# A four-layer graph network on one core: another order for the last six chunks of its attention stage

## The chip, the cores and the metric

The kernel runs on one core of a Trainium2 chip. The metric is device time in microseconds (us), the median of the runs shown. A core has five instruction queues that matter here: TensorE (PE in the profile), VectorE (DVE), ScalarE (ACT), GpSimd (POOL) and SyncE (SP), which issues the DMAs. Each queue is worked off strictly in order, and semaphores hold an instruction until what it reads is there and what it overwrites has been read.

## The reference

The input `x` is 128 graphs of 64 nodes with 256 features, all float32, and one 64 x 64 adjacency for all. Four layers follow each other, each as `x = x + layer(relu(layernorm(x)))`:

```python
# layer 0: graph convolution with two batch norms
# layer 1: two graph convolutions, then LSTMs over windows of 1, 2, 3 and 4 nodes
# layer 2: causal attention, one head
q, k, v = split(h @ Wqkv);  s = q @ k.T / 16 + adj;  s = where(causal, s, -1e30)
x = x + (softmax(s) @ v) @ Wo
# layer 3: attention with 4 heads of 64, masked where adj == 0
q, k, v = split(h @ W);     s = q @ k.T / 8 + (0 if adj else -inf)
x = x + softmax(s) @ v
```

The change touches only the last part of layers 2 and 3.

## The kernel before

The rows of `x` are cut into 16 chunks of 512 rows (8 graphs), and `x` stays on chip. Layers 0 and 1 end at about 1490 us. Then an attention stage takes each chunk through layers 2 and 3. It is written as some 50 small named steps (`q5`, `score3`, `turn3` and so on), each a function of the chunk number. Three strings say in which order the steps are recorded: FIRST once, ROUND eight times (chunks 4 to 11, some 21 us each), LAST once. A word `score3+13` in LAST is the step `score3` for chunk 13. The instructions stand under a manual schedule, so each engine's queue has them in the order of the words; nothing else reorders them.

What a chunk passes through, with the engine of each step and the line by which the profile shows it:

- Layer 2. `norm2` (statistics on VectorE, L159 and L160; an inverse square root on GpSimd, L99 and L100), `apply2` (nmr on VectorE, L185; four activations on ScalarE, L187), `chan2` (eight transposes on TensorE, L240; copies on VectorE and ScalarE). `sums2` makes four differences on GpSimd (L327 to L330) for a product of seven block products instead of eight: `wz`, `w5`, `w6`, `w3`, `w7`, `w4` (TensorE, L1773 and L1776) with copies on ScalarE (L1786), and additions on VectorE (L1789) in `w7`, `w11`, `w12`. Queries and values lie in `qv`. `score2` (TensorE, L1836; mask and maximum on VectorE, L1839 and L1648; subtraction on GpSimd, L1649), `exp2` (ScalarE), `divide2` (sum, reciprocal and product on VectorE, L1653, L1658, L1659), `turn2` (two transposes on TensorE, L1668; copy on ScalarE, L1672), `out2` (TensorE, L1867; VectorE adds to `xs`, L1870).
- Between the layers. `norm3a`, `norm3b`, `apply3` (L2003, L2004, L99, L185, L187), `square3` (VectorE transposes 32 x 32 squares, L286, and SP stores the result to DRAM, far_h<-mid, L261), `load3` (SP reads it back turned, hT<-far_h, four DMAs, L268), `keep` and `back` (SP stores `xs` and reads it back in another row order, far_x<-xs, L261, and x<-far_x, four DMAs, L279).
- Layer 3. `sums_h` (GpSimd, four differences), then `qa`, `q5`, `q6`, `q3`, `qc`, `qd` (TensorE, L1938) with `c11`, `c12` (VectorE), and `va`, `v5`, `v6`, `v3`, `v7`, `v4` (TensorE, L2062) with `v11`, `v12` (VectorE, L2075). `score3` (TensorE, L2025; VectorE, L2031 and L1648; GpSimd, L1649), `exp3`, `sum3`, `divide3`, `turn3` (eight transposes, two copies on ScalarE), `out3` (TensorE, L2142), `store` (VectorE, L2157, and one DMA out, L2158).
- Chunk 15 ends otherwise: plain products `q30`, `k30`, `q31`, `k31` (L1526), `v3a`, `v3b` (L1519), `score3h`, and the rest in two halves (`exp3a` to `storeb`; L2192, L2208, L2213, L2229, L2230).

Buffers are few: all PSUM products share eight banks; `x` (the row order for the output) has two buffers, so a third `back` waits until a `store` has read its predecessor; `td`, `td2`, `mid`, `qk` and layer 2's `hT` have one each, most others two.

Of the kernel before, what the change touches and what calls it, by code (L numbers as in the profile page):

```python
# [19 lines left out]
def kernel(  # L20
# [2203 lines left out]
    def store(c, t):  # L2224
# [3 lines left out]
        for r in range(2):  # L2228
# [16 lines left out]
               w11+1 sum3-3 v6-2 w12+1 v12-3 divide3-3 load3-1 qc-2 v5-2 v11-2 out2+0 v7-2 qd-2 sums2+2  # L2245
               back-3 norm3a+0 q3-2 norm3b+0 turn3-3 c12-2 v4-2 wz+2 apply3+0 score2+1 exp2+1 score3-2
               out3-3 store-3 divide2+1 w6+2 w5+2 qa-1"""
    LAST = """sums_h+10 va+10 turn2+12 square3+11 exp3+9 w11+13 back+9 v3+9 v11+10 w7+13 load3+11 sum3+9
              v5+10 v12+9 v6+10 q6+10 w3+13 w4+13 divide3+9 q5+10 norm2+14 w12+13 v7+10 turn3+9 qc+10
              c11+10 apply2+14 out2+12 norm3a+12 qd+10 back+10 v4+10 score2+13 q3+10 c12+10 norm3b+12 v3+10  # L2250
              sums_h+11 exp2+13 divide2+13 out3+9 store+9 va+11 score3+10 turn2+13 qa+11 chan2+14 apply3+12
              out2+13 v6+11 c11+11 q5+11 norm3a+13 sums2+14 wz+14 v5+11 q6+11 square3+12 norm2+15 v12+10
              q3+11 w5+14 w6+14 keep+12 exp3+10 qc+11 w3+14 sum3+10 w7+14 divide3+10 qd+11 load3+12 v7+11
              v3+11 c12+11 w4+14 back+12 turn3+10 v4+11 apply2+15 w12+14 v11+11 keep+13 sums_h+12 w11+14
              norm3b+13 score3+11 out3+10 qa+12 va+12 c11+12 q5+12 apply3+13 store+10 score2+14 v5+12
              chan2+15 q6+12 v11+12 keep+11 exp2+14 sums2+15 exp3+11 square3+13 divide2+14 back+11 q3+12
              v6+12 wz+15 v12+11 qc+12 turn2+14 v7+12 c12+12 sum3+11 w6+15 qd+12 w11+15 out2+14 load3+13
              score3+12 w5+15 v4+12 sums_h+13 w7+15 w3+15 divide3+11 qa+13 norm3a+14 w4+15 w12+15 norm3b+14
              exp3+12 turn3+11 sum3+12 score2+15 q5+13 apply3+14 out3+11 exp2+15 q6+13 q3+13 v3+12 va+13
              v5+13 store+11 divide3+12 turn3+12 v6+13 square3+14 divide2+15 c11+13 v12+12 turn2+15 qc+13  # L2260
              out2+15 norm3a+15 norm3b+15 v7+13 out3+12 qd+13 load3+14 v3+13 v4+13 c12+13 sums_h+14
              apply3+15 keep+15 score3+13 va+14 qa+14 square3+15 q5+14 store+12 v11+13 q6+14 v6+14 c11+14
              q3+14 v5+14 c12+14 exp3+13 qc+14 sum3+13 qd+14 divide3+13 load3+15 score3+14 v12+13 keep+14
              v7+14 exp3+14 v3+14 turn3+13 q30+15 v11+14 sum3+14 k30+15 q31+15 v12+14 divide3+14 k31+15
              turn3+14 score3h+15 out3+13 exp3a+15 sum3a+15 v3a+15 back+13 v4+14 divide3a+15 exp3b+15
              back+15 v3b+15 turn3a+15 out3+14 store+13 sum3b+15 divide3b+15 back+14 out3a+15 storea+15
              turn3b+15 store+14 out3b+15 storeb+15"""
    assert (NCH, SUP) == (16, 2)

    def run(order, c):  # L2270
        for name in order.split():
            i = max(name.find("+"), name.find("-"))
            steps[name[:i]](c + int(name[i:]))

    with tc.manual_schedule(engines={mybir.EngineType.PE, mybir.EngineType.DVE,
# [3 lines left out]
        for c in range(4, 12):  # L2279
            run(ROUND, c)  # L2280
        run(LAST, 0)
    close_l2()
# [49 lines left out]
```

## Time and profile before

| what | value |
|---|---|
| median of 3 runs | 1844.11 us (1843.9 to 1846.07) |
| the profiled execution | 1844.12 us; its span 1842.3 us |
| busy over the span | PE 98%, DVE 73%, ACT 58%, POOL 36% |
| granted TensorE clock | 0.998 |
| LAST: first matmul to end of span | 1724.98 to 1842.3 |

The first row is what a change is judged by; the profile shows one execution from its first to its last instruction, and 1.8 us lie around its span. A timeline line gives the start, the duration, the engine, the line, the operation with its operands' names, how many instructions are merged, and in brackets the idle time before it with its releaser. A duration is that of a pipelined instruction, so the distance between two starts says more of an engine's pace than the durations do. A line of the chain gives start, duration, and what worked or waited.

### The profile page before, as it was taken

The numbers are of one execution on the slowest core, as the hardware profiler recorded it, in microseconds if no ns is written. First come the engines' busy times: TensorE is split into PE (matmuls) and PEld (weight loads), VectorE is DVE, ScalarE is ACT, GpSimd is POOL, SyncE is SP. The second block draws the span as 40 slices with busy tenths as digits, with TensorE's granted clock in tenths as the row PEclk, the third lists the DMA queues.
The fourth block names the chain that finished last, engine by engine and source line by source line (L and its number), as shares of the span: only waits on it lengthen the run. The fifth ranks groups of instructions, "written<-read, shape, count | busy, mean of one in ns | idle before, by whom it ended". The sixth has DMA issues, their size and how long they took to land.

```text
span 1842.3 us, 41656 instructions
## 1 busy us (share of the span) xinstructions
PE 1812.8 (98%) x15847; PEld 1530.5 (83%) x15847; DVE 1353.4 (73%) x3475; ACT 1061.0 (58%) x2538; POOL 656.5 (36%) x916
## 2 busy tenths in 40 slices
PE   8999999999999999999999999999999999999997
PEld 6876866997897899799699789879968887998885
DVE  5768857567667777777777777777676677888997
ACT  5766636557457466665655746556565654554553
POOL 5865823223223322422321332232232215444442
PEclk9999999999999999999999999999999999999999
DMA  3213651233443342243443434324154146544444
GB/s 117 70 58 139 221 218 53 81 115 126 133 143 127 115 153 81 98 146 110 149 154 122 149 115 161 110 95 147 41 172 149 64 110 202 155 139 139 139 139 138
DMA packets 113416, 234.54 MB, mean 127 GB/s; under 512 B 11713, under 2 KB 77121, under 8 KB 113217
## 3 DMA queue, kind: packets, MB, share of 16 engines
q1 hardware_dynamic: 112320, 230.02, 38.3%
q8 instruction: 125, 2.05, 0.5%
q0 software_dynamic: 320, 1.05, 0.2%
q10 hardware_dynamic: 576, 0.82, 0.1%
q14 instruction: 75, 0.61, 0.1%
HBM read 164.21 MB, written 67.63 MB: 126 GB/s over the span
## 4 chain that ended last, share of the span: by engine, by line
PE 88%; DVE 5%; ACT 2%; POOL 2%; DMA 1%; issue 1%; SPq 0%; ACTq 0%; DVEq 0%; POOLq 0%
PE x L1186 23%; PE z L1186 11%; PE y L1186 6%; PE y L1133 4%; PE x L1368 4%; PE y L1368 3%; PE u L948 3%; PE v L934 3%; PE x L1133 3%; PE X L1938 2%; PE X L436 2%; PE X L512 2%; PE z L1133 2%; PE v L2062 2%; PE X L1773 1%
## 5 line engine op out<-in xcount | busy, mean ns | idle before, releaser
L1101 ACT ACTIVATE l_gates<-l_gates,bias 128x256 f32<-128x256 f32 (+4 forms) x528 | 238.1, 498 | 210.9 <-DVE l_gates L1195 109.7
L1186 PE MATMUL x<-xd,wset 128*128 128x128 f32 (+2 forms) x1152 | 254.9, 303 | 0.8 <-ACT l_gates L1192 0.8
L1186 PE MATMUL x<-l_hd,wset 128*128 128x128 f32 (+2 forms) x1152 | 254.6, 303 | 0.0
L1252 POOL TENSOR_TENSOR l_gates<-l_gates 128x512 f32<-128x512 f32 (+2 forms) x48 | 75.3, 1569 | 368.1 <-ACT l_gates L1101 368.1
L1195 DVE TENSOR_TENSOR l_gates<-l_gates,x 128x128 f32<-128x128 f32 (+2 forms) x384 | 121.1, 321 | 97.9 <-PE x L1186 95.2
L1186 PEld LDWEIGHTS x<-xd,wset 128*128 128x128 f32 x1152 | 187.7, 191 | 6.4 <-issue 1.4
L1186 PEld LDWEIGHTS x<-l_hd,wset 128*128 128x128 f32 x1152 | 187.7, 191 | 5.0
L1195 DVE TENSOR_TENSOR l_gates<-l_gates,z 128x128 f32<-128x128 f32 (+2 forms) x384 | 102.3, 318 | 105.4 <-PE z L1186 103.4
L1186 PE MATMUL z<-l_hs,wset 128*128 128x128 f32 (+2 forms) x768 | 147.1, 304 | 0.7 <-DVE l_hs L1110 0.7
L1186 PE MATMUL z<-hT,wset 128*128 128x128 f32 (+2 forms) x768 | 146.2, 303 | 0.0
L1192 ACT COPY l_gates<-y 128x128 f32<-128x128 f32 (+2 forms) x192 | 53.2, 290 | 137.7 <-PE y L1186 131.5
L1186 PEld LDWEIGHTS z<-l_hs,wset 128*128 128x128 f32 x768 | 116.7, 191 | 5.8 <-DVE l_hs L1110 2.5
L1186 PEld LDWEIGHTS z<-hT,wset 128*128 128x128 f32 x768 | 117.1, 191 | 3.3
L1101 ACT ACTIVATE l_gates<-x,bias 128x128 f32<-128x128 f32 (+2 forms) x216 | 84.8, 393 | 28.6 <-PE x L1186 25.9
L327 POOL TENSOR_TENSOR xd<-hT 128x128 f32<-128x128 f32 (+2 forms) x72 | 42.9, 596 | 127.5 <-DVE hT L1112 113.7
L1186 PE MATMUL x<-hT,wset 128*128 128x128 f32 (+2 forms) x384 | 85.8, 305 | 0.0
L1186 PE MATMUL x<-l_hs,wset 128*128 128x128 f32 (+2 forms) x384 | 84.9, 303 | 0.0
L1186 PE MATMUL y<-l_hd,wset 128*128 128x128 f32 (+2 forms) x384 | 83.2, 309 | 0.0
L1186 PE MATMUL y<-xd,wset 128*128 128x128 f32 (+2 forms) x384 | 81.6, 304 | 0.0
L1267 ACT ACTIVATE l_gates<-l_cell 128x256 f32<-128x256 f32 (+2 forms) x144 | 55.2, 384 | 45.7 <-DVE l_cell L1266 45.1
L328 POOL TENSOR_TENSOR xd<-hT 128x128 f32<-128x128 f32 (+3 forms) x80 | 51.5, 644 | 67.0 <-DVE hT L1116 29.5
L1110 DVE TENSOR_TENSOR l_hs<-l_gates 128x256 f32<-128x256 f32 (+4 forms) x120 | 51.4, 428 | 29.6 <-ACT l_gates L1159 13.8
(408 smaller groups left out, 4694.3 us busy)
## 6 DMA issues: line engine op xcount, KB each, us to landing
wset<-wfar SPq DMA_DIRECT2D x96, 896.0 KB, 8.2
hT<-far_h SPq DMA_DIRECT2D x124, 128.0 KB, 4.6
far_h<-hm SPq DMA_DIRECT2D x16, 512.0 KB, 3.0
far_n<-xs SPq DMA_DIRECT2D x16, 512.0 KB, 3.3
xs<-far_n SPq DMA_DIRECT2D x64, 128.0 KB, 2.8
far_x<-xs SPq DMA_DIRECT2D x16, 512.0 KB, 3.8
x<-far_x SPq DMA_DIRECT2D x64, 128.0 KB, 3.9
xt<-in_x_dram SPq DMA_DIRECT2D x15, 512.0 KB, 4.0
```

What stands on the lines that cost most here:

```text
L328: lambda: ((third or engine).tensor_tensor(t3, b22, b12, OP.subtract), engine.tensor_tensor(t2, b22, t1, OP.subtract)),
L934: nc.tensor.matmul(banks[m], wg0_sb[:, k, m * P : (m + 1) * P], agg[:, k, :], start=(k == 0), stop=(k == KD - 1))
L948: nc.tensor.matmul(banks[j // 2][:, j % 2, :], v[:, k, j * P : (j + 1) * P], wg1_sb[:, k, :], start=(k == 0), stop=(k == KD - 1))
L1101: nc.scalar.activation(gate(q, c, part), src, AF.Tanh if q == 2 else AF.Sigmoid, bias=bs[:, q * KD + c : q * KD + c + 1])
L1110: nc.vector.tensor_mul(hn[:, c, part], gate(3, c, part), gate(2, c, part))
L1133: nc.tensor.matmul(folded(self.psum(kind)), wsets[p, self.q][:, BLOCKS[kind][0], :], ox[0][kind], start=kind in (1, 5), stop=True, skip_gr ...
L1186: nc.tensor.matmul(folded(self.psum(kind)), wsets[p, self.q][:, BLOCKS[kind][i], :], (ox[self.s] if part == "x" else oh)[kind], start=firs ...
L1192: nc.scalar.copy(gate(self.q, kind // 5, halves[kind // 5]), self.psum(kind))
L1195: nc.vector.tensor_add(gate(self.q, *dst), gate(self.q, *a), self.psum(kind))
L1252: nc.gpsimd.tensor_mul(gates[:, 0, :, :n], gates[:, 0, :, :n], gates[:, 2, :, :n])
L1267: nc.scalar.activation(gate(2, c, part), cells[:, c, part], AF.Tanh)
L1368: nc.tensor.matmul(folded(ps(g, kind)), single_block(KINDS1[kind])[:, g, :], right[kind], start=kind in (2, 5, 1), stop=True, skip_group_c ...
```

## The change

Only the string LAST is replaced. It has the same 226 words as before in another order. FIRST, ROUND and every step are untouched. Some places, by the words around them:

- `norm3b+13` stands 10 words behind `out2+13`, where it stood 37 behind; `norm3a+15`, `norm3b+15`, `apply3+15` and `square3+15` stand before `score3+13`, where `square3+15` stood behind it.
- `load3+15` follows `c12+14`, ahead of `v6+14`, `qc+14` and `store+12`; it stood behind `store+12` and `divide3+13`.
- `score2+15` directly follows `norm3a+14` and `w4+15`; `turn3+11` is followed by `back+11`, `divide2+15` and `out3+11`; `turn2+15` by `divide3+12`, `q6+13`, `store+11`, `square3+14` and `out2+15`.
- `divide3+14`, `turn3+14`, `out3+14`, `v3+14` and `v12+14` stand in the very end, between the halves of chunk 15; `score3+14` stands between `q30+15` and `k30+15`, `turn3+13` before `score3h+15`; `store+13` comes before `sum3a+15`.

The diff, cut to the second half of LAST:

```diff
...
-              exp3+12 turn3+11 sum3+12 score2+15 q5+13 apply3+14 out3+11 exp2+15 q6+13 q3+13 v3+12 va+13
-              v5+13 store+11 divide3+12 turn3+12 v6+13 square3+14 divide2+15 c11+13 v12+12 turn2+15 qc+13
-              out2+15 norm3a+15 norm3b+15 v7+13 out3+12 qd+13 load3+14 v3+13 v4+13 c12+13 sums_h+14
-              apply3+15 keep+15 score3+13 va+14 qa+14 square3+15 q5+14 store+12 v11+13 q6+14 v6+14 c11+14
-              q3+14 v5+14 c12+14 exp3+13 qc+14 sum3+13 qd+14 divide3+13 load3+15 score3+14 v12+13 keep+14
-              v7+14 exp3+14 v3+14 turn3+13 q30+15 v11+14 sum3+14 k30+15 q31+15 v12+14 divide3+14 k31+15
-              turn3+14 score3h+15 out3+13 exp3a+15 sum3a+15 v3a+15 back+13 v4+14 divide3a+15 exp3b+15
-              back+15 v3b+15 turn3a+15 out3+14 store+13 sum3b+15 divide3b+15 back+14 out3a+15 storea+15
-              turn3b+15 store+14 out3b+15 storeb+15"""
...
+              turn2+14 v7+12 back+12 out2+14 w4+15 norm3a+14 score2+15 v4+12 norm3b+14 sums_h+13 exp3+12
+              exp2+15 sum3+12 keep+13 qa+13 turn3+11 back+11 divide2+15 out3+11 apply3+14 turn2+15
+              divide3+12 q6+13 store+11 square3+14 out2+15 turn3+12 q5+13 v3+12 keep+15 norm3a+15 norm3b+15
+              back+13 qc+13 va+13 v11+12 v5+13 q3+13 v6+13 load3+14 v3+13 apply3+15 v12+12 qd+13 c12+13
+              v7+13 c11+13 out3+12 v4+13 sums_h+14 square3+15 score3+13 qa+14 c11+14 va+14 q5+14 v11+13
+              q6+14 exp3+13 q3+14 c12+14 load3+15 v6+14 qc+14 v5+14 v11+14 keep+14 v12+13 sum3+13 v7+14
+              store+12 qd+14 q30+15 score3+14 k30+15 divide3+13 q31+15 k31+15 exp3+14 back+15 sum3+14
+              turn3+13 score3h+15 exp3a+15 v4+14 out3+13 exp3b+15 v3a+15 v3b+15 store+13 sum3a+15 v3+14
+              divide3a+15 divide3+14 sum3b+15 back+14 turn3a+15 out3a+15 divide3b+15 storea+15 v12+14
+              turn3+14 turn3b+15 out3+14 store+14 out3b+15 storeb+15"""
```

More of the change, by code (lines that the diff above doesn't have):

```diff
@@ L2247 @@
                out3-3 store-3 divide2+1 w6+2 w5+2 qa-1"""
[L2248 to L2258, printed above, removed]
-              exp3+12 turn3+11 sum3+12 score2+15 q5+13 apply3+14 out3+11 exp2+15 q6+13 q3+13 v3+12 va+13
-              v5+13 store+11 divide3+12 turn3+12 v6+13 square3+14 divide2+15 c11+13 v12+12 turn2+15 qc+13
-              out2+15 norm3a+15 norm3b+15 v7+13 out3+12 qd+13 load3+14 v3+13 v4+13 c12+13 sums_h+14
-              apply3+15 keep+15 score3+13 va+14 qa+14 square3+15 q5+14 store+12 v11+13 q6+14 v6+14 c11+14
-              q3+14 v5+14 c12+14 exp3+13 qc+14 sum3+13 qd+14 divide3+13 load3+15 score3+14 v12+13 keep+14
-              v7+14 exp3+14 v3+14 turn3+13 q30+15 v11+14 sum3+14 k30+15 q31+15 v12+14 divide3+14 k31+15
-              turn3+14 score3h+15 out3+13 exp3a+15 sum3a+15 v3a+15 back+13 v4+14 divide3a+15 exp3b+15
-              back+15 v3b+15 turn3a+15 out3+14 store+13 sum3b+15 divide3b+15 back+14 out3a+15 storea+15
-              turn3b+15 store+14 out3b+15 storeb+15"""
@@ new lines @@
+    LAST = """v3+9 w3+13 w11+13 square3+11 exp3+9 sums_h+10 load3+11 v12+9 turn2+12 w7+13 va+10 sum3+9
+              w12+13 q5+10 v5+10 c11+10 q6+10 w4+13 back+10 divide3+9 v3+10 v6+10 back+9 turn3+9 norm2+14
+              qc+10 v7+10 out2+12 qd+10 v4+10 apply2+14 norm3a+12 q3+10 sums_h+11 out3+9 c12+10 norm3b+12
+              v11+10 score2+13 chan2+14 store+9 va+11 keep+11 exp2+13 sums2+14 apply3+12 score3+10
+              divide2+13 q5+11 qa+11 wz+14 v6+11 v12+10 q3+11 keep+12 square3+12 turn2+13 q6+11 norm2+15
+              exp3+10 w5+14 load3+12 sum3+10 w6+14 v5+11 qc+11 v7+11 c12+11 c11+11 w3+14 qd+11 apply2+15
+              w12+14 divide3+10 v4+11 sums_h+12 w7+14 w11+14 out2+13 score3+11 w4+14 qa+12 norm3a+13 v3+11
+              turn3+10 q6+12 exp3+11 v11+11 norm3b+13 score2+14 out3+10 chan2+15 sum3+11 q5+12 apply3+13
+              store+10 qc+12 v12+11 va+12 sums2+15 divide3+11 c11+12 q3+12 square3+13 exp2+14 wz+15 v5+12
+              w11+15 w5+15 c12+12 divide2+14 w6+15 qd+12 w3+15 load3+13 w7+15 w12+15 v6+12 score3+12
+              turn2+14 v7+12 back+12 out2+14 w4+15 norm3a+14 score2+15 v4+12 norm3b+14 sums_h+13 exp3+12
[8 more added lines that the diff above has]
+              turn3+14 turn3b+15 out3+14 store+14 out3b+15 storeb+15"""
```

## The prediction

> **What bounds it now.** I read the busy table of the page first (TensorE: "PE 1812.8 (98%)"), then the busy time by stretch over LAST, then the timeline of LAST for TensorE's stops, then the chain that ended last. LAST's first matmul stands at 1724.98 and the span ends at 1842.3.
>
> ```profile
> core 0: us, PE busy (x) PEld busy (x) DVE busy (x) ACT busy (x) POOL busy (x), PEclk, DMA share, GB/s
> 1725.00:1745.00 20.00, 20.00 (x296) 17.70 (x295) 19.14 (x46) 9.99 (x21) 8.98 (x14) 1.00 0.50 150
> 1745.00:1765.00 20.00, 20.00 (x271) 18.02 (x270) 18.39 (x41) 12.18 (x24) 10.08 (x14) 1.00 0.44 144
> 1765.00:1785.00 20.00, 19.56 (x230) 16.76 (x229) 18.54 (x33) 9.83 (x20) 9.07 (x8) 1.00 0.41 132
> 1785.00:1805.00 20.00, 19.18 (x342) 16.33 (x341) 18.05 (x43) 11.30 (x24) 8.19 (x14) 1.00 0.32 108
> 1805.00:1815.40 10.40, 9.03 (x110) 7.22 (x108) 9.61 (x16) 3.95 (x7) 1.83 (x1) 1.00 0.61 198
> 1815.40:1842.30 26.90, 17.61 (x308) 12.08 (x308) 15.12 (x30) 7.78 (x14) 3.99 (x3) 0.89 0.41 120
> ```
>
> The reader sees two regimes: until 1815 both TensorE and VectorE are nearly full (VectorE idles 5.9 of the 80 us to 1805), then a tail in which no engine is.
>
> A busy matmul may still be waiting, so I count from starts. In unstopped runs of the timeline a matmul starts every 0.216 us (128x256), 0.112 (128x128), 0.109 (transpose), 0.429 (128x512), 0.035, 0.032, 0.017 and 0.016 (L1836, L1867, L2025, L2142). The counts of LAST times these are 99.8 us; first to last matmul start (1834.28) is 109.3. So TensorE stops for 9.6 us: 7.4 before the first matmul of q30+15 (1815.37), 2.2 after it. From its last matmul to the end it is 8.0 us more.
>
> ```profile
> 1794.27 0.41 PE L1668 MATMUL tr<-ident,s 128*128 128x128 f32 x2 [0.18 <-DVE s L1659]
> ...
> 1800.45 0.71 PE L2062 MATMUL v<-w_sb,td 128*128 128x128 f32 x4 [0.65 <-DVE v L2075]
> ...
> 1810.49 1.10 PE L1938 MATMUL X<-td,w_sb 128*128 128x256 f32 x4 [0.87 <-DVE qk L1985]
> ```
>
> (The bracket is idle time by modelled ends; by starts the three stops are 0.34, 0.81 and 1.11.) Of the 7.4 us, five stops make 3.5: 0.64 at 1767.6 (chan2+15 waits for a PSUM bank, freed by store+10 on VectorE), 0.34 (turn2+15 on divide2+15), 0.81 (v4+13 on v7+13's add), 1.11 (qd+14 on qc+14's add) and 0.61 (q30+15 on its load); four of 0.2 make 0.8 more. The other 3.1 are steps of about 0.1 at changes between full and split matmuls. The end, from the chain:
>
> ```profile
> 1804.77 1.42 DVE mid L286 x4
> 1806.21 4.54 DMA far_h<-mid
> ...
> 1812.13 3.10 DMA hT<-far_h
> 1815.23 0.14 issue
> 1815.37 1.95 PE p_q L1526 x4
> ...
> 1824.51 0.74 DVE s L2031 x2
> ...
> 1829.42 1.29 DVE o L2157 x2
> 1830.72 0.40 SPq L2158
> ...
> 1833.17 3.13 DMA x<-far_x
> ...
> 1836.42 0.69 DVE o L2157
> ```
>
> Chunk 15's square3 starts at 1804.77, its round trip through DRAM ends at 1815.2, and the last gate is x of chunk 14, whose buffer is free only once store+13 (L2157, 1829.42) has read x of chunk 13.
>
> **What the Trainium skill says.** "PSUM — Partial Sum Buffer", Specifications: 8 banks; the bank wait at 1767.6 agrees. "TensorEngine Tiling (Array Packing)", Key Properties: changing the tiling mode drains TensorE; the trace shows 0.09 to 0.10 us for it. "SBUF — State Buffer", Who interferes with whom: a VectorE instruction with two SBUF inputs and a GpSimd instruction that reads SBUF exclude each other wholly; agrees: L185 took 1.48 and 1.49 us (0.15 alone) and L1659 2.27 (1.22 alone), each under GpSimd's 1.90 us L1649. "DMA: Bandwidth & Descriptors", Two DMAs through the same engine are not ordered: a reload has to wait for the store's semaphore; agrees: load3+15 is issued only when the 4.54 us store has landed.
>
> **The change, part by part.** LAST keeps its 226 steps and only permutes them; the queues of the two programs hold the same instructions in new order. So busy times stay, and only stops and the tail move.
>
> (1) **Less TensorE work ahead of q30+15.** score3+14 (64 x 0.017 = 1.1), turn3+13 (8 x 0.109 = 0.87) and v3+14 (4 x 0.112 = 0.45) go behind its first matmuls: -2.4 us.
>
> (2) **Stops ahead of q30+15.** I followed the new queues with the durations above. Gone: the five stops and the four of 0.2, 4.3 us. Why: store+10 and the other users of tight banks now come four or more matmul groups ahead; divide2+15 is followed by out3+11 before turn2+15; out3+12 stands between v7+13 and v4+13; v5+14 and v7+14 between qc+14 and qd+14. New: score2+15 directly behind w4+15, whose ScalarE copy takes 0.59 plus about 0.2 to be seen: 0.8. out3+11 directly behind turn3+11, whose first copy is half covered: 0.4. sums_h+13 is on GpSimd's queue behind norm3b+14's rsqrt (1.3), and q6+13 needs its third difference: 0.3. turn2+15's copy is behind apply3+14 on ScalarE (4 x 0.5), so out2+15 waits 0.8 after q6+13. q5+13 takes the bank of turn3+12: 0.3. qd+14: 0.3. Sum 2.9. Net -1.4.
>
> (3) **Chunk 15's chain** must not be later than that. In TensorE's order out2+15 comes 5.7 us of matmuls earlier and its norm follows with no other chunk's square3 or scores between. score3+13's mask and maximum (1.28 + 1.22) are now behind square3+15 instead of ahead, and 1.9 us of small adds cover apply3+15. I get square3+15 at 1800 to 1802. On SP its store and load3+15 are neighbours: keep+14 and store+12 are behind. Before, store+12's output was issued in the 4.54 us; an earlier store (1793.18) was read back after 2.8. So the load lands 8.7 to 10.5 us after square3's start, 1809 to 1812. On SP back+13 is now ahead of load3+14, four issues of 0.47; its landing near 1800 is just in time for qa+14, cost 0 (up to 0.9 if late). So q30+15 stays TensorE-bound: 1815.4 - 2.4 - 1.4 = 1811.6.
>
> (4) **The tail.** Before, q30 to the first mask of score3h took 9.1 us; now score3+14 (1.1) stands in it and turn3+13 in place of turn3+14: 10.3, +1.2. From that mask VectorE's last add ended 13.9 us later, 2.7 of them waiting for x of chunk 14 (the add at 1836.42). Now store+13 comes ahead of sum3a, ending 3.8 after the mask and not 6.2, so x lands at 9.4; but divide3+14 (1.4), v12+14 (0.3) and turn3+14 are now in the tail. VectorE: 2.6 scores, 1.2 store+13, 1.5 first half, 1.4 divide3+14, 1.5 second half, 0.7 storea, 0.3 v12+14, 0.6 copy = 9.9; out3+14 then starts at 9.4 and ends at 10.4; store+14 and storeb end at 12.4: -1.5. The 3.9 after it (output DMA) stay. Net -0.3, from -1.5 to +1.5, as nothing in the old trace shows this crossing.
>
> **Sum.** -2.4 - 1.4 - 0.3 = -4.1. The profiled execution took 1844.12 (span 1842.3 and 1.8 around it), 0.01 off the median of 1844.11: 1840.0 us.
>
> **Rivals.** (a) **The stops return elsewhere.** Both engines are over 90% full in order, so a removed stop shows up at the next tight hand-over. Then only (1) is left, and the tail takes 1 of it back: 1844.1 - 2.4 + 1.0 = 1842.7. For it: VectorE's 5.9 us of idle. Against it: the removed stops have named causes that are now further apart. (b) **Late hand-overs make it slower.** The new places of (2) each put a consumer right behind its producer. If ScalarE or VectorE is a whole apply (2.1) later there, through the port lock (sums2+14, sums2+15, sums_h+12 and +13 now run beside divides and L185), each of five costs 2.4 instead of about 0.5: +9.4, 1840.0 + 9.4 = 1849.4. It decides from 7.0 us of stops at the new places on (2.9 + 4.1), and is slower by 0.2% from 10.7. For it: TensorE's queue there has only 0.9 to 4 us between producer and consumer; against it: VectorE has the same work and three of its lock waits (3.8 us) sat under exposed scores that now have other neighbours. (c) All new hand-overs are covered and the tail crosses cleanly: -2.4 - 4.3 - 1.0: 1836.4. (d) That it does nothing is excluded: every queue changes from its first steps in LAST.
>
> **Numbers.** 0.2% is 3.7 us, about what a measurement of this kernel can tell from no change. (my forecast) 0.42, (c) 0.12, (a) 0.30, (b) 0.16. My forecast's own range, 1838.0 to 1842.0, has its mean just past the 0.2% line (1840.4): I put the larger part of it on the faster side, since the two firmest terms, the work moved behind q30 and the earlier x, have no cost beside them. Faster 0.50, same 0.33, slower 0.17. The range leaves out the far ends of (b) and (c): 1836.0 to 1846.5.
>
> **What would show it.** Right: first p_q matmul near 1811.6, no wait of L2157 for x at the end, mid of chunk 15 near 1801, stops of 0.8 ahead of score2+15 and out2+15. Wrong: p_q at or after 1815, its load still the releaser; L185 or L1659 above 1.4 us more than three times; or the stretch from p_q to the end over 28 us (27 before).

## The result and the profile after

The kernel after takes 1841.74 us (median of 20 runs, 1840.95 to 1843.16) beside 1844.80 of the kernel before on the same chip: ratio 0.9983, 95% interval 0.9977 to 0.9989. That is 3.1 us or 0.17% less, clear of the noise. Its profiled execution took 1841.82 us with a span of 1839.9.

The busy time by stretch of the kernel after, with the columns and borders of the table of before (its last stretch ends with the span):

```profile
core 0: us, PE busy (x) PEld busy (x) DVE busy (x) ACT busy (x) POOL busy (x), PEclk, DMA share, GB/s
1725.00:1745.00 20.00, 20.00 (x296) 17.80 (x295) 18.99 (x44) 11.55 (x25) 11.17 (x17) 1.00 0.56 156
...
1785.00:1805.00 20.00, 18.14 (x311) 15.31 (x310) 17.18 (x38) 10.69 (x23) 9.19 (x12) 1.00 0.59 184
1805.00:1815.40 10.40, 9.73 (x106) 7.32 (x105) 6.36 (x12) 4.45 (x9) 1.90 (x1) 1.00 0.44 136
1815.40:1839.90 24.50, 17.36 (x316) 12.68 (x314) 18.65 (x31) 7.54 (x13) 3.99 (x3) 0.94 0.37 116
```

VectorE lost 3.2 us of work between 1805 and 1815.4 and gained 3.5 in the end, where score3+14 and divide3+13 now are. TensorE is less busy from 1785 to 1805 (18.14 for 19.18): four of the six larger new stops lie there. The timeline of the kernel after shows the three largest; for the last of them the two VectorE lines that lead to it stand ahead of it:

```profile
1788.82 1.13 PE L1938 MATMUL X<-td,ws 128*128 128x256 f32 x4 [0.71 <-POOL td L329]
...
1790.52 1.10 PE L1867 MATMUL o<-qv,att 64*32 64x256 f32 x32 [0.57 <-ACT att L1672]
...
1809.38 0.69 DVE L1985 TENSOR_TENSOR qk<-qk,X 128x512 f32<-128x512 f32 x1 [0.55 <-PE X L1938]
...
1809.99 0.41 DVE L2075 TENSOR_TENSOR v<-v,v 128x256 f32<-128x256 f32 x1
...
1810.46 0.71 PE L2062 MATMUL v<-wsv,td 128*128 128x128 f32 x4 [0.67 <-DVE v L2075]
```

By starts these cost 0.93 (q6+13 waits for GpSimd's third difference), 0.84 (out2+15 waits for turn2+15's copy) and 0.93 (v7+14). The last is a chain through two queues: v7+14 writes the PSUM bank that v11+14 still has to read; v11+14 stands on VectorE behind the add of qc+14 (L1985), which waits for qc+14's own matmuls.

The end, from the chain of the kernel after:

```profile
1812.03 1.72 PE p_q L1526 x4
...
1817.52 1.91 POOL s L1649
...
1825.63 1.28 DVE o L2157 x2
1826.91 0.02 issue
1826.93 0.40 SPq L2158
...
1829.37 4.45 DMA x<-far_x
...
1833.95 0.69 DVE o L2157
```

Chunk 15's store and reload have left the chain (before, they were 4.54 and 3.10 us of it): its mid is written at 1801.14, the reads are issued from 1805.34 on, the last of them has landed at 1811.34 (issued at 1806.64, 4.7 us in all), and q30+15 starts at 1811.87 without a wait, though with only 0.5 to spare. The last gate is still x of chunk 14.

**Where the time went.** The two executions enter LAST 0.63 us apart (first matmul 1724.98 before, 1724.35 after) with nothing changed ahead of it, so I count from that matmul:

| | before | after | |
|---|---|---|---|
| first matmul of LAST to first of q30+15 | 90.39 | 87.52 | -2.87 |
| of this, TensorE stopped | 7.3 | 6.9 | -0.46 |
| first matmul of q30+15 to end of span | 26.93 | 28.03 | +1.10 |

-2.87 is the moved work (2.42) and 0.46 of stops. (The stops are what is left of the stretch when the counted matmuls are taken off.) In this pair of profiles LAST gives 1.8 us; the medians differ by 3.1. The rest is the 0.63 ahead of LAST, where nothing was changed and where the fourteen profiles of this case spread from 1724.07 to 1725.58, and 0.7 by which the profiled execution of the kernel before (1844.12) lies under its median of 20 runs.

### The profile page after: what moved, and what is told of

Same layout as the page of the kernel before. It is cut to its first block, busy times and chain, and to the rows that moved or that the text cites. A ratio compares the mean times of both kernels' runs of the same rounds, so it can differ in the third digit from the quotient of the medians.

```text
span 1839.9 us, 41662 instructions
## 1 busy us (share of the span) xinstructions
PE 1813.3 (99%) x15847; PEld 1531.8 (83%) x15847; DVE 1353.8 (74%) x3475; ACT 1061.4 (58%) x2538; POOL 656.8 (36%) x916
## 3 DMA queue, kind: packets, MB, share of 16 engines
q8 instruction: 125, 2.05, 0.5%
## 4 chain that ended last, share of the span: by engine, by line
PE 89%; DVE 5%; ACT 2%; POOL 2%; issue 1%; DMA 0%; SPq 0%; DVEq 0%; ACTq 0%; POOLq 0%
PE x L1186 23%; PE z L1186 11%; PE y L1186 6%; PE y L1133 4%; PE x L1368 4%; PE y L1368 3%; PE u L948 3%; PE v L934 3%; PE x L1133 3%; PE X L1938 3%; PE X L436 2%; PE X L512 2%; PE v L2062 2%; PE z L1133 2%; PE Y L1938 1%; PE X L1773 1%
```

## Experiments

All were timed in five rounds beside the kernel before. "To q30" and "end" are the two stretches of the table above; the last column is the median less that of the kernel before in the same job (the kernel after: -3.1). The 95% intervals of the ratios below are two to five us wide, so small differences between two rows are read from the profiles, and each of these is a single execution.

| run | to q30 | end | median - before |
|---|---|---|---|
| x1_old_order_new_end | 90.43 | 27.79 | +1.5 |
| x1b_and_square_ahead | 89.65 | 27.78 | -0.6 |
| x1c_and_reload_ahead | 88.37 | 27.45 | -1.5 |
| x2_new_order_old_end | 91.44 | 29.52 | +2.2 |
| m_three_stops_mended | 88.03 | 26.92 | -3.3 |
| y1_v11_and_divide_ahead | 86.82 | 27.50 | -3.6 |
| y2_x_ahead_of_output | 87.54 | 27.82 | -3.0 |
| z1_both_gates | 87.54 | 27.48 | -3.4 |
| y3_all_covered | 86.11 | 27.09 | -4.8 |
| z2_all_covered_both_gates | 86.29 | 27.22 | -5.2 |
| z3_square_behind_out | 90.11 | 27.19 | -1.65 |
| w1_reload_behind_output | 95.32 | 30.45 | +7.4 |

### The old order with the new end

```diff
-qd+14 divide3+13 load3+15 score3+14 v12+13 keep+14 v7+14 exp3+14 v3+14 turn3+13 q30+15
+qd+14 load3+15 back+13 v12+13 keep+14 v7+14 v11+14 q30+15
```

(Behind q30+15 the steps of the kernel after.)

> The order of the kernel before up to q30+15, and behind it the end of the kernel after: score3+14, exp3+14, divide3+13, turn3+13 and v3+14 stand behind q30+15 (back+13 and v11+14 ahead of it). Chunk 15's square3 stays where it was (about 1804.8, its reload back at about 1815). Theory (the reload of chunk 15 was as late as TensorE, so that moving work behind q30 is worth nothing unless the chain comes earlier as well): the first p_q matmul stays at 1814.5 to 1815.5, now with a wait of about 2.5 us for the load ahead of it, the end behind it lasts 28.0 as in the kernel after, so 1844.8 + 0.6 = 1845.4 (1844.5 to 1846.5). Rival (TensorE's amount of work ahead of q30 is what counts): p_q at 1813.0, and with 1.1 more at the end 1843.5.

Measured: 1846.48, ratio to before 1.0009 (1.0002 to 1.0016). The first line of q30 in its timeline:

```profile
1815.61 1.95 PE L1526 MATMUL p_q<-hT,w_sb 128*128 128x512 f32 x4 [3.36 <-DMA hT<-far_h]
```

TensorE had 2.4 us less to do and by starts waited 3.5 for the reload instead (0.61 before). Moving the work alone is worth nothing (90.43 for 90.39) and lengthens the end. The theory held, at the upper end of its range. Part of the +1.5 may be the clock: the two fastest of the 21 executions (1843.76 and 1844.00) have a mean granted clock of 1.000, the two slowest (1848.45 and 1849.11) one of 0.997.

### Chunk 15's chain ahead

```diff
-keep+15 score3+13 va+14 qa+14 square3+15 q5+14
+keep+15 square3+15 score3+13 va+14 qa+14 q5+14
```

> As x1_old_order_new_end, and square3+15 moved ahead of score3+13, so that the mask and maximum of score3+13 (2.5 us of VectorE) are behind chunk 15's chain. Theory: square3+15 starts 2.5 us earlier (about 1802.3), its reload is back at about 1812.7, and p_q starts there: 1844.8 - 2.6 + 1.1 = 1843.3. Rival (the moved work counts whatever the chain does): the same time as x1_old_order_new_end within 0.5 us. Second rival (the delayed mask comes to stand in TensorE's way, because turn3+13 and the banks of scores wait on it): slower than x1_old_order_new_end by 1 us or more.

Measured: 1844.43, ratio 0.9997 (0.9989 to 1.0005), 2.05 below x1 by the medians, as the theory had it. In the two profiles it is less: from LAST's start square3+15 came 1.4 sooner (78.39 for 79.80; it waited 1.65 for apply3+15's activations on ScalarE) and q30 0.8, still behind the reload. The sign is shown, the size lies between 0.8 and 2, and the clock in x1's slow executions may be the difference. SyncE's own lines in the timeline of x1b (start, time of issue) show what was left:

```profile
1803.91 0.34 SPq L261 DMA_DIRECT2D far_h<-mid  x1
1807.53 0.39 SPq L2158 DMA_DIRECT2D out_dram<-o  x1
1808.03 2.82 SPq L268 DMA_DIRECT2D hT<-far_h  x4
```

The reads stand behind the output of store+12. So next load3+15 was put in front of it:

```diff
-square3+15 score3+13
+square3+15 load3+15 score3+13
```

(and load3+15 taken out behind qd+14)

> As x1b_and_square_ahead, and load3+15 moved from behind qd+14 to right behind square3+15, so that SyncE issues it ahead of the output of store+12, which in x1b went out at 1807.53 and pushed the four reads to 1808.03, 4.1 us after the issue of their store. Theory (the reload is the bound of x1b, with a TensorE wait of 1.28 ahead of p_q): the reads go out 2.7 to 3.0 after the store's issue, as in the kernel after, so at about 1806.8, and p_q starts 1.2 earlier at 1812.5, now bound by TensorE: x1b's 1844.4 - 1.2 = 1843.2. Rival (the store itself takes 4 us there, whatever SyncE does): no change from x1b within 0.3.

Measured: 1843.24, ratio 0.9993 (0.9985 to 1.0001); q30 came 1.28 sooner and no longer waits for a DMA. The reads went out 2.75 after the store's issue (1804.52 and 1807.27). The theory held. The other order has its price: in the profile of x1c qa+14 stops for 0.93 until score3+13's mask (L2031), which now stands behind square3+15 on VectorE, has read its bank; the kernel after has no stop there.

The reverse, the kernel after with load3+15 behind store+12:

```diff
-c12+14 load3+15 v6+14 qc+14 v5+14 v11+14 keep+14 v12+13 sum3+13 v7+14 store+12 qd+14
+c12+14 v6+14 qc+14 v5+14 v11+14 keep+14 v12+13 sum3+13 v7+14 store+12 load3+15 qd+14
```

> The kernel after with one step back: load3+15 behind store+12 (as in the kernel before, where store+12 stood much earlier), all else as in the kernel after. In the kernel after the output of store+12 goes out at 1813.41, once v7+14's add and store+12's own adds are done on VectorE. Theory (SyncE issues in order, so the four reads stand behind that output although chunk 15's store landed at about 1805.2): reads issued from 1813.9 to 1815.6, the last one 3.1 later at 1818.7, p_q there instead of at 1811.87: 1841.7 + 6.9 = 1848.6. Rival (VectorE, relieved of nothing, and TensorE lose no more than the slack of about 2 us, because the work behind q30 can't be reached but the store's adds come earlier when TensorE waits): 1844 to 1846.

Measured: 1851.95, ratio 1.0042 (1.0028 to 1.0056). The reads were issued from 1813.77 on and q30 started at 1819.45, 7.6 us after TensorE was ready: 0.7 later than the sum said; so far the theory held. The time came out another 2.6 longer, and the busy time by stretch of this run says why (the third number from the end of a row is PEclk, the granted clock):

```profile
1811.90:1815.20 3.30, 0.00 (x0) 0.00 (x0) 1.28 (x3) 0.56 (x1) 0.00 (x0) 1.00 0.32 109
1815.30:1825.50 10.20, 6.05 (x69) 3.43 (x70) 0.33 (x1) 0.59 (x1) 0.00 (x0) 0.50 0.51 117
1825.60:1828.00 2.40, 2.40 (x7) 1.01 (x6) 2.33 (x5) 0.59 (x1) 0.21 (x1) 1.00 0.00 0
```

From 3.4 us into the stop until 1825.5 TensorE was granted half its clock. By starts, the four matmuls of q30 took 3.68 instead of 1.81 and score3+14 1.92 instead of 1.09. The end is 2.4 us longer than that of the kernel after.

### The new order with the old end

```diff
-v7+14 store+12 qd+14 q30+15
+v7+14 store+12 qd+14 divide3+13 score3+14 exp3+14 v3+14 turn3+13 q30+15
```

(Behind q30+15 the steps of the kernel before, less v11+14 and back+13, which are ahead already.)

> The order of the kernel after up to q30+15, and behind it the end of the kernel before: divide3+13, score3+14, exp3+14, v3+14 and turn3+13 stand ahead of q30+15 (v11+14 and back+13 stay ahead of it too). Theory: chunk 15's reload is back at about 1810 and waits for TensorE, which has 2.4 us more to do: p_q at 1811.9 + 2.4 = 1814.3, plus up to 0.7 if turn3+13 waits for its divide; the end behind it lasts 27 as in the kernel before: 1841.7 + 2.4 - 1.1 = 1843.0 (to 1843.8). Rival (the gain of the change lies in the order up to q30 alone): within 0.5 of the kernel after, 1841.7. Second rival (it lies in the end alone): as the kernel before, 1844.8.

Measured: 1847.25, ratio 1.0012 (1.0005 to 1.0018): slower than before, outside both rivals and past the theory's 1843.8. To q30 it is 3.9 longer than the kernel after: the 2.42 of work, 0.98 because turn3+13 now waits for its softmax, and smaller stops. The end is 2.6 longer than that of the kernel before: turn3+14 stops TensorE for 0.81 (0.07 before), and x of chunk 14 keeps L2157 waiting 4.49 (2.73), its last read taking 4.59 for 3.13. In these forms neither half of the change alone is faster than before. Part of x2's loss is its own, though, as turn3+13 now stands close behind divide3+13.

### The stops that the prediction had missed or priced too low

Three edits, in one run (m) and then two of them alone (y1):

```diff
-v6+14 qc+14 v5+14 v11+14 keep+14
+v6+14 v11+14 qc+14 v5+14 keep+14
...
-qd+14 q30+15 score3+14 k30+15 divide3+13 q31+15
+qd+14 divide3+13 q30+15 score3+14 k30+15 q31+15
...
-w4+15 norm3a+14 score2+15 v4+12 norm3b+14 sums_h+13
+w4+15 v4+12 norm3a+14 norm3b+14 score2+15 sums_h+13
```

> The kernel after with three stops of TensorE mended by order alone: v11+14 ahead of qc+14 (so that v7+14 doesn't wait for an add that stands behind another wait, 0.93); norm3b+14 directly behind norm3a+14 and v4+12 between w4+15 and score2+15 (score2+15's stop 0.71 shrinks by 0.45, and GpSimd gets to the operands of q6+13 0.8 us sooner, 0.93); divide3+13 ahead of q30+15 instead of behind k30+15 (its L1659 of 2.87 us runs ahead of GpSimd's L1649 instead of under it, and turn3+13's stop of 0.72 goes). Theory (TensorE is the bound up to q30, chunk 15's reload lands about 2 us earlier): p_q at 1811.9 - 0.9 - 0.45 - 0.8 = 1809.8, where the reload begins to be the bound, and the end 0.7 shorter: 1841.7 - 2.8 = 1838.9. Rival (the removed stops return at the next hand-over, VectorE being over 90% full up to 1800): p_q no earlier than 1811.4, only the end gains: 1841.0. Second rival (a reload that has landed only just in time): p_q at 1811.0 with the reload as its releaser: 1840.2.

Measured: 1841.70, ratio 0.9982 (0.9974 to 0.9990), as the kernel after. The stops at q6+13 and v7+14 were gone and the one at score2+15 was 0.2, but one of 2.17 came up ahead of out3+11 (0.51 in the kernel after). The timeline of this run:

```profile
1785.19 1.04 POOL L100 TENSOR_TENSOR rstd_n<-rstd_n,mhalf 128x4 f32<-128x4 f32 x1
1786.20 0.61 POOL L1649 TENSOR_TENSOR s<-s,mx 128x256 f32<-128x256 f32 x1
1786.85 0.42 ACT L1846 ACTIVATE s<-s 128x256 f32<-128x256 f32 x1 [2.57 <-POOL s L1649]
...
1787.64 1.08 ACT L1672 COPY att<-tr 128x512 f32<-128x512 f32 x2
...
1788.28 1.18 PE L2142 MATMUL o<-v,att 64*64 64x64 f32 x64 [2.01 <-ACT att L1672]
```

The earlier inverse square root (L100) pushed score2+15's subtraction on GpSimd, that pushed exp2+15 on ScalarE, and turn3+11's copies stand behind exp2+15. The stop then cost more than its length, for TensorE was granted half its clock in what followed:

```profile
1788.30:1789.60 1.30, 1.30 (x66) 1.23 (x67) 1.27 (x4) 0.90 (x2) 1.22 (x2) 1.00 0.00 0
1789.70:1793.00 3.30, 3.30 (x38) 1.64 (x36) 3.30 (x6) 2.33 (x6) 0.16 (x1) 0.50 0.02 5
1793.10:1796.00 2.90, 2.66 (x24) 2.15 (x17) 2.83 (x9) 1.31 (x3) 0.00 (x0) 1.00 1.03 378
```

So q30's 88.03 holds both, a stop that came back and slow matmuls: out2+15 took 1.77 by starts instead of 1.03. The clock isn't all of it. Four of m's 14 executions have a mean granted clock of 1.000, which leaves no room for such a stretch (it alone would make it 0.999), and they took 1841.08 to 1841.76. The first rival held by the time, with this addition: what was removed came back at the next hand-over, and only the end gained (26.92).

> The kernel after with two of the three mends of m_three_stops_mended: v11+14 ahead of qc+14, divide3+13 ahead of q30+15. The norm of chunk 14 stays where it was (in m its early rsqrt on GpSimd pushed the subtraction of score2+15 from 1784.08 to 1786.20, and the copies of turn3+11 behind the exponential on ScalarE with it: a new stop of 2.17 ahead of out3+11). Theory (these two stops are removed and nothing takes their place): v7+14's 0.93 is gone, p_q at 1811.0 where the reload has just landed; L1659 of divide3+13 takes 1.2 to 1.4 instead of 2.87 and turn3+13's 0.72 is gone: 1841.7 - 0.9 - 0.7 = 1840.1. Rival (divide3+13 in front of q30 makes VectorE late for qd+14 or v7+14): p_q not earlier than 1811.9, 1841.0. Second rival (the tail is bound by x of chunk 14, whatever TensorE does): x's wait grows by what the stops give, 1841.3.

Measured: 1841.14, ratio 0.9982 (0.9975 to 0.9989), by the medians 0.5 to 0.6 below the kernel after where the theory had 1.6; the two intervals lie on each other, so the times alone don't show a gain. In the profile both stops are gone and q30 comes 0.70 sooner from LAST's start, so the first rival fell. The end is 0.5 shorter and no more, as x of chunk 14 now makes L2157 wait 1.04 (0.92): part of the second rival. The VectorE product of divide3+13 and GpSimd's subtraction, first in the kernel after, then in y1:

```profile
1817.52 1.90 POOL L1649 TENSOR_TENSOR s<-s,mx 128x1024 f32<-128x1024 f32 x1 [10.39 <-DVE mx L1648]
1817.63 2.87 DVE L1659 TENSOR_TENSOR s<-s,rs 128x1024 f32<-128x1024 f32 x1
```

```profile
1814.50 1.23 DVE L1659 TENSOR_TENSOR s<-s,rs 128x1024 f32<-128x1024 f32 x1
```

In the kernel after the product starts 0.11 behind the subtraction and takes 1.65 us longer than alone. That is the 0.72 by which turn3+13 stopped TensorE; the profile there names exp3+14 (L2122), which ended 0.01 later.

### The gates of the end

```diff
         for r, ps in enumerate(st.pop((c, "o3"))):
             nc.vector.tensor_add(pairs(o, r), pairs(st[c, "x"], r), ps)
-        nc.sync.dma_start(outr[c], o)
+        st[c, "out"] = o
+        if c != 13:
+            steps["putout"](c)
+
+    @step
+    def putout(c):
+        nc.sync.dma_start(outr[c], st[c, "out"])
...
-back+14 turn3a+15
+back+14 putout+13 turn3a+15
```

> The kernel after with one change of SyncE's queue: the reads of x of chunk 14 (four of 128 KB) are issued ahead of the output of chunk 13 (512 KB), once store+13's adds are done. Theory (the reads took 4.45 us because the output of 512 KB that was issued 0.5 ahead shared the DMA engines): the last read takes about 3.1, is issued 0.5 sooner, and x has landed 1.8 sooner; L2157 of store+14 then waits for the products of out3+14 instead and starts about 0.5 sooner: 1841.2. Rival (the reads are slow by themselves): they still take 4.4, land 0.5 sooner, and the add starts 0.4 to 0.5 sooner; the time is the same, the read's duration tells the two apart. Second rival (the output, now issued behind the reads, ends last or is in the way of the last outputs): 1842 or more.

Measured: 1841.74, ratio 0.9986 (0.9979 to 0.9992), no change. The reads landed in 2.6 us (median of the four; 4.2 in the kernel after), so the output ahead of them had slowed them; yet the add started within 0.15 of where it had been, counted from q30. Its chain:

```profile
1828.80 4.99 DMA out_dram<-o
...
1833.91 0.69 DVE o L2157
```

The second rival, in a form I had not thought of: store+14's o takes over the buffer of chunk 13's o, so it waits until that output has left. Without this gate too:

```diff
-        o = l2.tile([P, NJ, D], F32, tag="o", name=f"o_{c}")
+        o = st[c, "x"] if c == 14 else l2.tile([P, NJ, D], F32, tag="o", name=f"o_{c}")
```

> y2_x_ahead_of_output, and store+14 adds in place into x of chunk 14 instead of into a new o. In y2 the reads of x landed in 2.6 us and not 4.45, but the add then waited for the output of chunk 13 (issued at 1828.80, 4.99 us): o of chunk 14 takes over the buffer of o of chunk 13. Theory (the end of the kernel after has two gates behind store+13, the reads of x and the buffer of o; only without both does the add start with its products): no wait of L2157 for a DMA, it starts at about 1833.4 instead of 1833.95 (the products of out3+14 end at 1833.3): 1841.7 - 0.5 = 1841.2. Rival (the end is bound by TensorE and VectorE, and the gates come no later than the products): 1841.7, the add's start as in y2 within 0.1.

Measured: 1841.60, ratio 0.9983 (0.9977 to 0.9990). From q30's first matmul to the add of store+14 it is 21.56 us (22.08 in the kernel after), so the 0.5 is there, and no DMA is waited for:

```profile
1834.48 1.28 DVE L2157 TENSOR_TENSOR x<-x,o 128x512 f32<-128x512 f32 x2 [0.39 <-PE o L2142]
```

The times can't tell 0.5 from 0. So in the profile the two gates cost the kernel after 0.5; past that the products of out3+14 set the end.

### All together

```diff
-w4+15 norm3a+14 score2+15 v4+12 norm3b+14
+w4+15 v4+12 norm3a+14 score2+15 norm3b+14
...
-turn2+15 divide3+12 q6+13 store+11 square3+14 out2+15
+turn2+15 va+13 divide3+12 q6+13 v3+12 store+11 square3+14 out2+15
```

(va+13 and v3+12 taken from their places behind out2+15; with the edits of y1 and y2)

> The kernel after with both mends of y1_v11_and_divide_ahead, the reads ahead of the output of y2_x_ahead_of_output, and three hand-overs covered by other matmuls: v4+12 between w4+15 and score2+15 (0.45 of its 0.71), va+13 between turn2+15 and q6+13 (0.9 of 0.93), v3+12 between q6+13 and out2+15 (0.45 of 0.84). Theory (each stop counts one for one as long as chunk 15's reload keeps ahead, and it comes earlier with out2+15): 0.45 + 0.9 + 0.45 + 0.93 = 2.7 off p_q (1809.1), 0.7 + 0.5 off the end: 1841.7 - 3.9 = 1837.8. Rival (VectorE and ScalarE are what sets the pace at 1780 to 1795, and the stops return at the next hand-over, as in m): only the mends of y1 and y2 are left: 1839.6. Second rival (chunk 15's reload becomes the bound): p_q at 1810.0, with the load as its releaser: 1838.7.

Measured: 1839.87, ratio 0.9975 (0.9965 to 0.9984); between the theory and the first rival. To q30 it gained 1.41, not 2.7: the stops at score2+15, q6+13 and out2+15 fell from 2.5 to 0.5, but the second half of turn3+12 now waits 1.08 for the bank that out2+15's adds free on VectorE (q5+13 had 0.46 there), and a new stop of 0.47 stands ahead of turn2+15.

> y3_all_covered with the add in place of z1_both_gates. In y3 the add of store+14 started at 1832.01, 0.68 of idle time ahead of it put down to the output of chunk 13; the products of out3+14 end at about 1831.5. Theory: 0.4 to 0.5 sooner, 1839.9 - 0.45 = 1839.4. Rival: as in z1, no change, 1839.9.

Measured: 1839.83, ratio 0.9971 (0.9960 to 0.9983), as y3; the 0.45 did not show. These two are the fastest found, 1.9 us below the kernel after and 5 below the one before; the slowest of their 17 executions (1840.78) is faster than the fastest of the kernel after (1840.95). A last attempt at the 1.08:

```diff
-store+11 square3+14 out2+15 turn3+12
+store+11 out2+15 square3+14 turn3+12
```

> z2 with square3+14 behind out2+15. In y3 the second half of turn3+12 waited 1.08 us for the PSUM bank of o2_15, which the adds of out2+15 (L1870) free; they ran at 1792.67, behind store+11 (1.27) and the transposes of square3+14 (1.41) on VectorE, while TensorE had the products ready at 1792.0. Theory (VectorE's order sets this hand-over): the adds start at 1792.0, turn3+12's stop shrinks by 0.7, chunk 15's norm and its reload come 0.7 sooner too, p_q 0.7 sooner: 1839.4 - 0.7 = 1838.7. Rival (chunk 14's reload, now stored 1.3 later and read behind the four reads of x, is late for qa+14 at 1802.2 and for GpSimd's operands, which waited for it already): the stop comes back there, 1839.4 or more.

Measured: 1843.39, ratio 0.9989 (0.9981 to 0.9998). turn3+12's stop halved (0.52), and qa+14 then waited 2.6 us for chunk 14's reload, with the TensorE clock at 0.50 for the 3.4 us behind it. The rival held, and dearer than it had said. (Three of the 13 executions took 1841.2 to 1841.6, the others 1842.8 to 1844.7; what sets the three apart is open.)

## Why the prediction was right or wrong

**Right in direction, 1.7 us too low** (1840.0; 1841.74 measured, inside the forecast's own 1838 to 1842, but the gain is 0.17%, short of the 0.2% that it had given the better odds). There is some luck in it. In LAST, the only part that the forecast is about, the profiles show -1.8 for its -4.1; that alone would be 1842.3. And q30 at 1811.87 seems close to the forecast 1811.6 because LAST began 0.63 sooner: from its first matmul it is 87.52 for 86.6.

(1) Work behind q30: held, 2.42 by the count of the matmuls. x1 adds the condition: without (3) it is worth nothing, since the reload was as late as TensorE. The prediction took (3) as a check that must not fail; it was what let the gain through. Step by step q30 went 90.39, 90.43 (work moved), 89.65 (square3+15 ahead), 88.37 (reload ahead of the output), 87.52 (the rest of the order): 2.1 of the 2.9 came only with chunk 15's chain.

(2) **Stops, net -1.4 forecast, -0.46 measured: the step that failed.** The five large old stops had gone. Of the new ones score2+15 (0.71 for 0.8), out3+11 (0.51 for 0.4), out2+15 (0.84 for 0.8) and q5+13 (0.46 for 0.3) were right. q6+13 was priced at 0.3 and took 0.93: GpSimd's inverse square root and three differences took 3.6 us from the last statistics (1785.17 to 1788.76), longer than the sum had left for them. v7+14's 0.93 was not seen; the walk through the queues had put 0.3 at qd+14, where none was, since it followed what each step needs but not the bank that v11+14 keeps. Together the new stops came to 4.4 for a forecast 2.9. That the net is still -0.46 is due to the many small steps, which fell from about 3.0 to 2.5; they were not followed one by one.

(3) Chunk 15's chain: held. square3+15 at 1801.14 (1800 to 1802), reads issued 2.75 after the store, the last landed at 1811.34 (1809 to 1812). It held narrowly, 0.5 ahead of q30.

(4) **The end, -0.3 forecast, +1.1 measured.** q30 to the first mask took 10.98 for 10.3: divide3+13's product (L1659) ran under GpSimd's L1649, a lock that the prediction had quoted and counted only in a rival; in y1, where the product runs ahead, this stretch is 10.34. From mask to last add it was 13.0 for 12.4: the last read of x took 4.45, not the 3.13 of the old trace, with 0.5 MB of output issued just ahead. The sum had x land as out3+14 began. z1 says how much of it that cost: 0.5. (The sum's list of VectorE's work adds up to 9.8, not 9.9; nothing hangs on that.) Two of the signs named in advance went against it: L2157 did wait for x (0.92), and the stretch from q30 to the end, 28.03, just passed the bound of 28.

Of the rivals, (a) is the nearest to what happened, at 1842.7: part of the stops came back. Not (b): the late hand-overs cost 4.4 in all, under its 7.0, and L185 or L1659 took more than 1.4 us three times in LAST (L1659 1.69, 1.55 and 2.87), as often as before.

## What to carry to other kernels

When an engine and a DMA chain end together, moving work away from the engine is worth nothing until the chain comes earlier too; look for what stands ahead of the chain's last transfer on the issuing queue (here an output that no one waits for). When stops are priced on an almost full schedule, follow for every hand-over not only the data but the buffer or bank and who still has to read it, and expect part of what is removed to come back at the next one. Here that part varied: in the change itself 4.3 us went and 4.4 came, in m all came back (with a halved clock), in y3 about half of 2.7, in y1 a quarter of 0.93. Price a last transfer with what is issued just ahead of it (2.6 or 4.2 us here), and allow for the clock behind a stop of 2 us or more.

## What the runs showed of the hardware

- A stop of TensorE can cost more than its length. In m a stop with 2.0 us of idling was followed, 1.4 us after its end, by 3.4 us at a granted clock of 0.50; in z3 one with 2.6 us was followed at once by 3.4 us at 0.50; in w1 the clock went to 0.50 after 3.4 of the 7.6 us, for 10.2 us, of which TensorE worked 6.1. After 3.4 us in the profiled execution of x1 it stayed at 1.00. The Trainium skill, "TensorE: Matmul & The Clock Gate", What's actually happening, says that the clock is halved after an idle window of about 3.4 us and that the window runs freely. The length of the slow stretches and w1 agree with that, and x1 can, as its stop may have lain across two windows; m and z3 halved after shorter gaps, so a gap under 3.4 us is not safe.
- Four reads of 128 KB took 2.6 us to land (median) with nothing issued just ahead and 4.2 behind an output of 512 KB (y2 and the kernel after); the output took 5.0 behind the reads and 3.2 ahead of them. Why the last read behind an output took 3.1 in the kernel before and 3.9 to 4.6 in eight others (the kernel after, x1, x1b, x1c, x2, m, y1, w1) is open.
